# A run of four row gathers is put behind VectorE's one-hots of the next batch, three batches ahead, in place of TensorE's factors of the next batch, four ahead

## The chip, the cores and the metric

The kernel runs on one core of one Trainium2 chip. The core has five engines with queues of their own: PE (TensorE, matmuls), DVE (VectorE), ACT (ScalarE), POOL (GpSimd) and SP (SyncE, which here only issues transfers). The metric is the time of the program on the device in microseconds, the median of several executions.

## The reference

One message-passing block of a graph network, then a layer norm over the sum of the input and the block's output. There are 1250 nodes with 512 values each (384 of them three-component vectors `v`, 128 scalars `s`), and 40000 edges, sorted by their target node `dst`.

```python
x_j = x[src]
v_j = x_j[:, :384].reshape(E, 128, 3)
s_j = silu(x_j[:, 384:] @ W1 + b1) @ W3 + b3
edge_basis = rbf * cutoff @ W2 + b2
split = s_j * edge_basis
s1, s2, s3 = (split[:, :128], split[:, 128:256], split[:, 256:])
v_msg = v_j * s1[:, :, None] + s3[:, :, None] * edge_attr1[:, None, :]
msg = jnp.concatenate([v_msg.reshape(E, 384), s2], axis=1)
x = x + jax.ops.segment_sum(msg, dst, num_segments=N_NODES)
```

After this first sum each node's new row is put through an update (matrices `U`, `V`, `Wu1`, `Wu2`), and a second sum adds the updated rows over the same edges. What the second sum adds depends on the source node alone.

## The kernel before

**Tiling.** `windowed()` does the whole work. The edges are cut into 79 chunks of 512, four chunks make a group, and there are 20 groups. A group is worked on in four batches; a batch has one tile of 128 edges from each of its chunks, so four tiles in nearly all batches, three in batch 76 and two in the last three. There are NT = 80 batches and 313 tiles. An edge needs one row of a table in DRAM, which was made beforehand for every node: 640 values, the vector part with the scalar part after its two matmuls.

**The loop.** Step t of the loop at L1677 stands for batch t. What the steps do around the change, in the order of the program:

- `messages(t)` (DVE): L899 and L901 multiply the gathered rows by the edges' factors, in place, in the room where the rows were put. Then come `make_pair(t)` (L919), `make_hot(t + 1)` (L830, a one-hot matrix of the edges' targets within a 16-node window, for the next batch) and `make_spread(t + 1)` (L842, the same times the edge's direction).
- `run(first, t)`: work that a planner has set down for this step, of node blocks and of the second sum. `run(early)`, `run(mid)`, `run(late)` and `run(dve)` are more of it, further on in the step.
- `add_messages(t - 1)` and `count_links(t - 1)` (PE): matmuls of the one-hots with the messages of the batch before, L935 and L941, and of link counts for the second sum, L964.
- `edge_factors(t + 1)` (PE, L889): eight matmul records for four tiles into one set of PSUM banks, named `eb`. There is one such set, so these matmuls wait until L901 of batch t has read it. L899 of batch t + 1 waits for them.
- `gather(t + 4, made)`: a run of four indirect DMAs on POOL's queue (L739), each of 128 rows. `made` is the last matmul of `edge_factors(t + 1)`, and the run's first gather has a dependency on it that is written by hand (L748); the other three stand behind the first in POOL's queue.

The gathered rows go to five rooms in turn, three in the buffer `more` and two in `nodes`, which is why the profile lists L739, L899 and L901 under two names. The gathers of batches 0 to 3 are issued ahead of the loop, without a dependency by hand, and so are those of the last two batches at their places.

**What else sets the order.** The program's order is each engine's order. Across engines an instruction waits for what it reads and for the last reader of what it writes; only the dependencies by hand are added. `after_factors` (L1053) makes SP's transfers of node parts wait for `made` as well, the newest factors at the time when they are put into the program. POOL has other work near the end alone: a memset, casts of link counts, sums of parts of the output.

Of the kernel before, what the change touches and what calls it, by code (L numbers as in the profile page):

```python
# [64 lines left out]
def gnn_resnorm(  # L65
# [315 lines left out]
    with tc.If(misses_v == 0):  # L381
        windowed(tc, sh)
# [201 lines left out]
def windowed(tc, sh):  # L584
# [13 lines left out]
    nc = tc.nc  # L598
# [12 lines left out]
    def lanes(g, i, j):  # L611

        c = g * CPG + j
        if c >= NCH:
            return 0
        n = CHUNK if c < NCH - 1 else last_rows
        return max(0, min(P, n - i * P))
# [3 lines left out]
    NT = len(batches)  # L621

    def tiles(g, i):
        return [j for j in range(CPG) if lanes(g, i, j)]

    def runs(g, i):

        out = []
        for j in tiles(g, i):
            if out and lanes(g, i, out[-1][-1]) == lanes(g, i, j):  # L630
                out[-1].append(j)
            else:
                out.append([j])
        return [(slice(js[0], js[-1] + 1), len(js), lanes(g, i, js[0])) for js in out]
# [13 lines left out]
    with tc.tile_pool(  # L648
# [80 lines left out]
        sync = mybir.DependencyInfo(mybir.DependencyClass.Sync, mybir.DependencyReason.DATA)  # L729

        rooms = itertools.cycle(sh.rooms)

        def gather(t, behind=None):

            g, i = batches[t]
            rows_t = next(rooms)
            for j in tiles(g, i):
                n = lanes(g, i, j)
                got = nc.gpsimd.indirect_dma_start(  # L739
                    out=rows_t[:n, j, :],  # L740
                    out_offset=None,
                    in_=sh.table1,
                    in_offset=bass.IndirectOffsetOnAxis(
                        ap=sh.src_i[:n, g, i * CPG + j : i * CPG + j + 1], axis=0
                    ),
                )
                if behind is not None and j == 0:
                    tc.add_manual_dep(  # L748
                        got.ins, behind.ins.name, sync,
                        reason="so that rows come while PE is ahead of DVE",  # L750
                    )
            clear_rest(t, rows_t, nc.gpsimd)
            rows_of[t] = rows_t
# [59 lines left out]
        def clear_rest(t, tile, engine=nc.vector):  # L813
            g, i = batches[t]
            for j in tiles(g, i):
                m = lanes(g, i, j)
                if m < P:
                    engine.memset(tile[m:, j], 0.0)

        def make_hot(t):  # L820

            g, i = batches[t]
            hots[t] = pool.tile([P, CPG, WIN], F32, name="hot", bufs=3)
            spread[t] = pool.tile([P, CPG, 3, WIN], F32, name="spread", bufs=3)
            clear_rest(t, hots[t])
            clear_rest(t, spread[t])
            for js, n, m in runs(g, i):
                e = i * CPG + js.start
                shape = [m, n, WIN]
                nc.vector.tensor_tensor(  # L830
                    hots[t][:m, js, :],
                    lane[:m, None, :WIN].to_broadcast(shape),
                    sh.local[:m, g, e : e + n, None].to_broadcast(shape),
                    op=ALU.is_equal,
                )

        def make_spread(t):
            g, i = batches[t]
            for js, n, m in runs(g, i):
                e = i * CPG + js.start  # L840
                shape = [m, n, 3, WIN]
                nc.vector.tensor_mul(  # L842
                    spread[t][:m, js],
                    hots[t][:m, js, None, :].to_broadcast(shape),
                    sh.attr[:m, g, e : e + n, :, None].to_broadcast(shape),
                )
# [11 lines left out]
        def mark_sources(t):  # L858

            g, i = batches[t]  # L860
            for j in tiles(g, i):
                e = g * EPG + i * CPG + j
                one = onehots[t][:, j, :]
                nc.scalar.activation(  # L864
                    one, one, AF.Relu, scale=less[:, e : e + 1], bias=worth[:, e : e + 1]
                )
# [5 lines left out]
        def new_banks(name, sizes):  # L872

            factor_banks.close()
            banks.push(factor_banks)
            of = factor_banks.enter_context(tc.tile_pool(name=name, bufs=1, space=PSUM))
            return [
                of.tile([P, n, BANK], F32, name=f"{name}_{k}") for k, n in enumerate(sizes)
            ]

        def factors_of(t, js):

            return made_in[t][:, js]

        def edge_factors(t):
            g, i = batches[t]
            for j in tiles(g, i):
                rows = slice(j * FEAT, j * FEAT + N_RBF + 1)
                made = nc.tensor.matmul(  # L889
                    made_in[t][:, j, :V], turned[g][rows, i, :], sh.w2_sb[rows, :],  # L890
                    start=True, stop=True,
                )
            return made

        def messages(t):
            g, i = batches[t]
            msg = rows_of.pop(t)
            for js, n, m in runs(g, i):
                nc.vector.tensor_mul(msg[:m, js, V:], msg[:m, js, V:], factors_of(t, js)[:m, :, C:V])  # L899
            for js, n, m in runs(g, i):  # L900
                nc.vector.tensor_mul(  # L901
                    msg[:m, js, :V].rearrange("p t (k c) -> p t k c", k=3),
                    msg[:m, js, :V].rearrange("p t (k c) -> p t k c", k=3),
                    factors_of(t, js)[:m, :, None, :C].to_broadcast([m, n, 3, C]),
                )
            make_pair(t)
            if t + 1 < NT:
                make_hot(t + 1)
                make_spread(t + 1)
            msgs[t] = msg  # L910

        def make_pair(t):

            g, i = batches[t]
            pair = pool.tile([P, CPG, PARTS * WIN], F16, name="pair", bufs=2)
            for js, n, m in runs(g, i):
                e = g * EPG + i * CPG + js.start
                shape = [m, n, PARTS * WIN // 2, 2]
                nc.vector.tensor_tensor(  # L919
                    pair[:m, js, :].rearrange("p t (l h) -> p t l h", h=2),  # L920
                    number[:m, : PARTS * WIN].rearrange("p (l h) -> p l h", h=2)[
                        :, None
                    ].to_broadcast(shape),
                    column[:m, e : e + n, None, :].to_broadcast(shape),
                    op=ALU.is_equal,
                )
            pairs[t] = pair
# [688 lines left out]
        def run(when, step):  # L1616
            for _, fn, args in sorted(when.get(step, []), key=lambda task: task[0]):
                fn(*args)
# [49 lines left out]
            at(early, 4 * g - 3, 6, bring_fades, g)  # L1668
        distances(0)
        mark_sources(0)  # L1670
        ahead = 4
        for t in range(min(ahead, NT)):
            gather(t)
        edge_factors(0)
        make_hot(0)
        make_spread(0)
        for t in range(max(*first, *early, *late, *dve, *mid) + 1):  # L1677
            if t < NT:
                messages(t)
            if t == NT - 4:  # L1680
                assert all(len(tiles(*batches[u])) == CPG // 2 for u in range(NT - 3, NT))
                made_in[NT - 3], made_in[NT - 2] = new_banks("halves", [CPG // 2] * 2)
                made_in[NT - 1] = made_in[NT - 3]
            if t == NT - 1:
                out_banks.update(zip(in_factors, new_banks("out", [1] * CPG), strict=True))
            run(first, t)
            if 1 <= t <= NT:
                add_messages(t - 1)
                count_links(t - 1)
            run(early, t)  # L1690
            if t + 1 < NT - 2:
                made = edge_factors(t + 1)
            if t + 1 in (NT - 3, NT - 2):
                edge_factors(t + 2)
            if t + ahead < NT:
                gather(t + ahead, made if t + ahead < NT - 2 else None)
            run(mid, t)
            run(late, t)
            run(dve, t)
# [368 lines left out]
```

## Time and profile before

| | us |
|---|---|
| median of 3 executions | 582.91 (582.26 to 584.65) |
| the profiled execution | 581.79 |
| its span, from the first to the last instruction | 579.9 |
| first L899 into the room `nodes` | 62.8 |
| last L899 into the room `nodes` | 518.1 |

The mean granted clock of TensorE was 0.902 in the profiled execution. A row of a timeline has the start of an instruction in us from the span's start, its duration in us, the engine, the line, the operation with out<-in and the tile's shape, and in brackets how long the engine was idle before it and what ended that. A group's row has the count, the busy time, the mean duration in ns, and the idle time before its instructions with the most frequent releaser. A row of a window has its two ends, its length, the busy time and count of each engine in the order PE, PE's weight loads, DVE, ACT, POOL (or of one engine alone), TensorE's granted clock, the DMA engines' busy share and GB/s. Ends of matmuls are modelled, so what follows a matmul is read from the waiting instruction's start.

### The profile page before, as it was taken

To read this page: it belongs to the slowest core of one execution; us is meant where nothing else is said; L and a number is where in the kernel's file an instruction comes from. 1 tells how busy PE (TensorE), PEld (TensorE's weight loads), DVE (VectorE), ACT (ScalarE), POOL (GpSimd) and SP (SyncE) were. 2 spreads that over 40 slices of the span, in tenths; PEclk is the share of its full clock that TensorE was granted. 3 is DMA by queue.
4 is the path that set the end of the run, shared out by engine and by line. 5 is a ranking of instruction groups with operands and counts; after the bars stand their busy time and mean duration, and the time that the engine had idled before them with its cause. 6 is when DMAs were issued, how large, how long until landed. Compare 5 with 4: busy or idle time off the path is not lost.

```text
span 579.9 us, 11213 instructions
## 1 busy us (share of the span) xinstructions
PE 458.1 (79%) x4233; PEld 254.6 (44%) x4233; DVE 437.1 (75%) x680; ACT 372.5 (64%) x946; POOL 332.9 (57%) x361
## 2 busy tenths in 40 slices
PE   6566777769768778977778697889789887989993
PEld 3322432335335334534434353454445444445682
DVE  6893778767776877778778867788778686878775
ACT  3470466557656676856667685677668675877664
POOL 6375666655555656656566655566565655653530
PEclk9956787889887998989799889889989998999998
DMA  7986777775766777777677777777777776765514
GB/s 225 303 239 213 212 233 213 213 227 172 237 191 192 235 223 216 216 241 208 201 230 224 216 218 207 223 222 244 224 225 200 247 234 194 230 198 185 189 37 148
DMA packets 37937, 123.28 MB, mean 213 GB/s; under 512 B 7296, under 2 KB 9870, under 8 KB 37874
## 3 DMA queue, kind: packets, MB, share of 16 engines
q0 software_dynamic: 25824, 104.47, 60.5%
q1 hardware_dynamic: 10574, 17.24, 9.0%
q10 hardware_dynamic: 1476, 0.77, 0.5%
q8 instruction: 35, 0.57, 0.4%
q14 instruction: 28, 0.23, 0.1%
HBM read 112.94 MB, written 9.51 MB: 211 GB/s over the span
## 4 chain that ended last, share of the span: by engine, by line
PE 32%; POOL 21%; issue 17%; DVE 14%; DMA 8%; ACT 5%; another core or an unknown queue 2%; DVEq 0%; POOLq 0%; ACTq 0%; SPq 0%
POOL more L739 12%; POOL nodes L739 7%; PE agg L935 6%; PE eb L889 6%; PE agg L941 4%; PE begun L1339 4%; DMA more<-table,src_i 3%; DMA nodes<-table,src_i 3%; DVE nodes L901 2%; DVE more L901 2%; PE adj L964 2%; PE work L806 2%; DVE nodes L899 2%; DVE more L899 2%
## 5 line engine op out<-in xcount | busy, mean ns | idle before, releaser
L739 POOL DMA_INDIRECT more<-table,src_i x189 | 183.9, 973 | 127.1 <-issue 46.2
L739 POOL DMA_INDIRECT nodes<-table,src_i x124 | 119.3, 962 | 80.0 <-issue 28.7
L864 ACT ACTIVATE one<-one,weight,src_f 128x128 f16<-128x128 f16 x313 | 128.5, 482 | 0.4 <-issue 0.2
L889 PE MATMUL eb<-w_sb,basis_t 21*128 21x384 f32 x614 | 83.2, 561 | 42.9 <-issue 18.3
L854 ACT ACTIVATE one<-number,low 128x128 f16<-128x128 f16 x313 | 99.7, 391 | 5.5 <-remote 3.9
L901 DVE TENSOR_TENSOR more<-more,eb 128x1536 f32<-128x1536 f32 (+2 forms) x48 | 81.8, 1705 | 0.0
L899 DVE TENSOR_TENSOR more<-more,eb 128x1024 f32<-128x1024 f32 (+2 forms) x48 | 57.0, 1190 | 31.3 <-PE eb L889 13.5
L935 PE MATMUL agg<-more,hot 128*32 128x512 f32 x378 | 67.1, 697 | 3.3 <-ACT sums L986 2.1
L889 PEld LDWEIGHTS eb<-w_sb,basis_t 21*128 21x128 f32 x614 | 28.2, 189 | 69.5 <-issue 33.5
L941 PEld LDWEIGHTS agg<-more,spread 128*32 128x32 f32 x1134 | 42.6, 122 | 35.8 <-issue 34.3
L941 PE MATMUL agg<-more,spread 128*32 128x128 f32 x1134 | 53.2, 300 | 2.0 <-issue 1.9
L901 DVE TENSOR_TENSOR nodes<-nodes,eb 128x1536 f32<-128x1536 f32 x30 | 52.4, 1747 | 0.0
L935 PE MATMUL agg<-nodes,hot 128*32 128x512 f32 x248 | 44.0, 688 | 6.2 <-ACT sums L986 3.8
L842 DVE TENSOR_TENSOR spread<-hot,carried 128x384 f32<-128x384 f32 (+1 forms) x81 | 44.0, 544 | 2.8
L899 DVE TENSOR_TENSOR nodes<-nodes,eb 128x1024 f32<-128x1024 f32 x30 | 36.5, 1216 | 11.7 <-DMA more<-table,src_i 8.2
L964 PE MATMUL adj<-pair,one 128*128 128x160 f16 x313 | 39.0, 249 | 2.5 <-issue 2.5
L1010 DVE SCALAR_TENSOR_TENSOR counts<-counts,adj 128x320 f16<-128x320 f16 x20 | 9.7, 486 | 40.9 <-ACT counts L1004 28.8
L941 PEld LDWEIGHTS agg<-nodes,spread 128*32 128x32 f32 x744 | 28.0, 123 | 25.5 <-issue 25.1
L919 DVE TENSOR_TENSOR pair<-number,column 128x640 f16<-128x640 f16 (+1 forms) x81 | 38.2, 472 | 0.0
L941 PE MATMUL agg<-nodes,spread 128*32 128x128 f32 x744 | 35.7, 302 | 2.4 <-issue 2.4
L811 ACT COPY basis_t<-work 128x512 f32<-128x512 f32 x20 | 11.7, 586 | 35.9 <-PE work L806 32.6
L964 PEld LDWEIGHTS <-one 128*128 128x128 f16 x313 | 24.0, 107 | 15.0 <-issue 13.4
(274 smaller groups left out, 717.6 us busy)
## 6 DMA issues: line engine op xcount, KB each, us to landing
table<-more SPq DMA_DIRECT2D x10, 320.0 KB
more<-table,src_i POOLq DMA_INDIRECT x189
spilled<-begun SPq DMA_DIRECT2D x10, 256.0 KB
more<-spilled SPq DMA_DIRECT2D x2, 1280.0 KB
node_x<-in_x_dram SPq DMA_DIRECT2D x35, 64.0 KB
nodes<-table,src_i POOLq DMA_INDIRECT x124
out_dram<-more SPq DMA_DIRECT2D x7, 256.0 KB
nodes<-in_x_dram POOLq DMA_DIRECT2D x2, 768.0 KB
```

Of the source, the lines that this page charges most:

```text
L739: got = nc.gpsimd.indirect_dma_start(out=rows_t[:n, j, :], out_offset=None, in_=sh.table1, in_offset=bass.IndirectOffsetOnAxis(ap=sh.src_i ...
L842: nc.vector.tensor_mul(spread[t][:m, js], hots[t][:m, js, None, :].to_broadcast(shape), sh.attr[:m, g, e : e + n, :, None].to_broadcast(sh ...
L854: nc.scalar.activation(onehots[t][:, j, :], number[:, :P], AF.Abs, bias=low[:, e : e + 1])
L864: nc.scalar.activation(one, one, AF.Relu, scale=less[:, e : e + 1], bias=worth[:, e : e + 1])
L889: made = nc.tensor.matmul(made_in[t][:, j, :V], turned[g][rows, i, :], sh.w2_sb[rows, :], start=True, stop=True,)
L899: nc.vector.tensor_mul(msg[:m, js, V:], msg[:m, js, V:], factors_of(t, js)[:m, :, C:V])
L901: nc.vector.tensor_mul(msg[:m, js, :V].rearrange("p t (k c) -> p t k c", k=3), msg[:m, js, :V].rearrange("p t (k c) -> p t k c", k=3), fac ...
L919: nc.vector.tensor_tensor(pair[:m, js, :].rearrange("p t (l h) -> p t l h", h=2), number[:m, : PARTS * WIN].rearrange("p (l h) -> p l h", ...
L935: nc.tensor.matmul(agg[j * WIN : (j + 1) * WIN, :], hots[t][:, j, :], msg[:, j, :width], start=(i == 0), stop=False, skip_group_check=True,)
L941: nc.tensor.matmul(agg[j * WIN : (j + 1) * WIN, c * C : (c + 1) * C], spread[t][:, j, c, :], msg[:, j, width:], start=False, stop=(i == la ...
L964: nc.tensor.matmul(to[:, :, at : at + WIN], one[:m, j, :], pair[:m, j, :].rearrange("e (p n) -> e p n", n=WIN), start=(i == 0 and j == js[ ...
L1339: nc.tensor.matmul(acc, casts[a, b], rows[:, a, :], start=(start and a == first and k == 0), stop=(stop and a == end - 1 and k == 1),)
```

## The change

A run of gathers is moved within the step, from behind `edge_factors(t + 1)` to right behind `messages(t)`. Its first gather depends on two instructions: `made`, which is at that place the last matmul of `edge_factors(t)`, and `gate`, the one-hots that `make_hot(t + 1)` makes on DVE. The run in step t is that of batch t + 3, not t + 4, and three runs stand ahead of the loop, not four. The last two batches' runs have no dependency by hand, as before. `messages` and `make_hot` return the instruction for it.

```diff
-        def gather(t, behind=None):
+        def gather(t, behind=()):
...
-                if behind is not None and j == 0:
+                for made in behind if j == 0 else ():
                     tc.add_manual_dep(
-                        got.ins, behind.ins.name, sync,
-                        reason="so that rows come while PE is ahead of DVE",
+                        got.ins, made.ins.name, sync,
+                        reason="so that rows come while PE makes a batch's factors",
                     )
...
-                nc.vector.tensor_tensor(
+                made = nc.vector.tensor_tensor(
                     hots[t][:m, js, :],
...
+            return made
...
+            gate = None
             make_pair(t)
             if t + 1 < NT:
-                make_hot(t + 1)
+                gate = make_hot(t + 1)
                 make_spread(t + 1)
             msgs[t] = msg
+            return gate
...
-        ahead = 4
+        ahead = 3
         for t in range(min(ahead, NT)):
             gather(t)
-        edge_factors(0)
+        made = edge_factors(0)
         make_hot(0)
         make_spread(0)
         for t in range(max(*first, *early, *late, *dve, *mid) + 1):
             if t < NT:
-                messages(t)
+                gate = messages(t)
+            if t + ahead < NT:
+                gather(t + ahead, (made, gate) if t + ahead < NT - 2 else ())
...
             if t + 1 in (NT - 3, NT - 2):
                 edge_factors(t + 2)
-            if t + ahead < NT:
-                gather(t + ahead, made if t + ahead < NT - 2 else None)
```

## The prediction

> **What bounds the kernel now.** I read the page's busy shares first, then its costliest groups, and last the timelines of PE, DVE and POOL over two steps in the middle.
>
> ```profile
> span 579.9 us, 11213 instructions
> PE 458.1 (79%) x4233; PEld 254.6 (44%) x4233; DVE 437.1 (75%) x680; ACT 372.5 (64%) x946; POOL 332.9 (57%) x361
> L739 POOL DMA_INDIRECT more<-table,src_i x189 | 183.9, 973 | 127.1 <-issue 46.2
> L739 POOL DMA_INDIRECT nodes<-table,src_i x124 | 119.3, 962 | 80.0 <-issue 28.7
> L899 DVE TENSOR_TENSOR more<-more,eb 128x1024 f32<-128x1024 f32 (+2 forms) x48 | 57.0, 1190 | 31.3 <-PE eb L889 13.5
> L899 DVE TENSOR_TENSOR nodes<-nodes,eb 128x1024 f32<-128x1024 f32 x30 | 36.5, 1216 | 11.7 <-DMA more<-table,src_i 8.2
> ```
>
> No engine is full, and DVE's idle time in front of L899 (31.3 + 11.7 us) is put down to PE's factors (`eb`) in one group and to a gather in the other. So the question is what sets the length of a step. The windows, all engines first and then L899 alone, give its mean:
>
> ```profile
> 63.00:518.00 455.00, 366.24 (x3665) 198.44 (x3669) 346.75 (x486) 305.84 (x786) 274.48 (x285) 0.91 0.73 218
> 63.00:518.00 455.00, 86.24 (x71) 0.91 0.73 218
> ```
>
> 71 steps in 455 us are 6.41 us each; DVE works 346.75/71 = 4.88 us of that. Three timelines of one step, DVE's, PE's and POOL's:
>
> ```profile
> 287.07 1.22 DVE L899 TENSOR_TENSOR nodes<-nodes,eb 128x1024 f32<-128x1024 f32 x1 [0.60 <-DMA more<-table,src_i]
> 288.21 1.75 DVE L901 TENSOR_TENSOR nodes<-nodes,eb 128x1536 f32<-128x1536 f32 x1
> 290.28 0.28 DVE L830 TENSOR_TENSOR hot<-lane,carried 128x128 f32<-128x128 f32 x1
> 293.25 1.22 DVE L899 TENSOR_TENSOR nodes<-nodes,eb 128x1024 f32<-128x1024 f32 x1 [1.31 <-DMA more<-table,src_i]
> ```
>
> ```profile
> 286.08 0.93 PE L889 MATMUL eb<-w_sb,basis_t 21*128 21x384 f32 x8
> 290.21 0.93 PE L889 MATMUL eb<-w_sb,basis_t 21*128 21x384 f32 x8
> ```
>
> ```profile
> 287.31 0.94 POOL L739 DMA_INDIRECT more<-table,src_i  x1 [3.16 <-PE eb L889]
> 291.05 0.94 POOL L739 DMA_INDIRECT more<-table,src_i  x1 [0.30 <-issue]
> 293.49 0.94 POOL L739 DMA_INDIRECT more<-table,src_i  x1 [1.49 <-remote]
> 299.55 0.94 POOL L739 DMA_INDIRECT nodes<-table,src_i  x1 [1.39 <-remote]
> ```
>
> The factors started at 286.08 let L899 go at 287.07, 0.99 us later, with no gather under way. The same eight matmuls started at 290.21, inside a run of gathers (287.31 to 291.05 + 0.94 = 291.99), let L899 go only at 293.25, 3.04 us later: 1.26 us after the run's last gather and 5.94 us after its first. That L899's own rows had been asked for four steps before; the "DMA" named as its releaser is the last event, not the cause. I read it so: **PE's signals are held while a run's rows stream, until about 5.9 us after the run's start.** The run in its turn starts 0.24 us after the factors' release (287.31 less 287.07). So a quiet step is a closed loop of 0.25 + 5.9 = 6.15 us: factors, run, held factors (287.07, 293.25, and runs at 293.49 and 299.55, 6.06 apart).
>
> Is 5.9 us the stream's own price? At the start 20 gathers are issued without a stop:
>
> ```profile
> 26.86 1.21 POOL L739 DMA_INDIRECT more<-table,src_i  x1 [9.07 <-DMA u_sb<-in_L_gnn_U_dram]
> 52.20 0.95 POOL L739 DMA_INDIRECT nodes<-table,src_i  x1 [0.30 <-issue]
> 56.34 1.22 DVE L899 TENSOR_TENSOR more<-more,eb 128x1024 f32<-128x1024 f32 x1 [9.01 <-PE eb L889]
> 48.44 0.79 PE L889 MATMUL eb<-w_sb,basis_t 21*128 21x384 f32 x1 [1.15 <-issue]
> 55.51 0.79 PE L889 MATMUL eb<-w_sb,basis_t 21*128 21x384 f32 x1 [0.42 <-issue]
> ```
>
> From 26.86 to 56.34 are 29.5 us, so at most 1.47 us a gather and 5.9 us for four. PE crawls there: eight factor matmuls spread from 48.44 to 55.51, and DVE stands idle 9.01 us.
>
> **The change part by part.** *The wait.* The new run waits for the one-hots of the next batch. L830 ends 290.28 + 0.28 - 287.07 = 3.49 us after L899 starts; with the 0.25 us to POOL's start as above, the run starts 3.75 us after L899 instead of 0.24. Behind the waiting gather stand on POOL the run's other three and the later runs, nothing else before the tail. The other wait, for this step's factors, is met already, since L899 needed them: 0. The run is put ahead of PE's work of the step in the program, but POOL's own queue holds the same gathers in the same order in the loop: 189 + 124 = 313 gathers, before and after, 291.99 - 287.31 = 4.68 us a run, and with the 0.30 between two gathers 4.98 from run to run at the least. The next factors start after L901 (288.21 + 1.75 = 289.96) at 290.21 at the earliest, and would signal 0.99 later, some 3.9 to 4.1 us after L899, which is 0.2 to 0.4 us after the new run's start. There the stream has hardly begun, the first gather's 0.94 us being still under way, and I take them to be released on time. So the next L899 no longer waits for the end of this run.
>
> *What is late next.* DVE has 4.88 us a step, POOL 4.98, the stream 5.9. If the stream is the next bound, a step is 5.9: it loses the 0.25 us between factors and run, which the new gate takes out of the loop, since the one-hots come (3.75 us) well before the last run has been served. Below that stand 4.98 (POOL), above it 6.15 (no gain), and beyond that a hold, priced with the rivals. I take 5.9, the row at the start being the nearest to runs without a gap.
>
> *The steps that gain.* In 14 of the 71 steps the factors start over 1.1 us after L901, since PE waits for chains of other work. The first and the last of the 14, L901 and then the factors:
>
> ```profile
> 113.61 1.75 DVE L901 TENSOR_TENSOR more<-more,eb 128x1536 f32<-128x1536 f32 x1
> 486.83 1.75 DVE L901 TENSOR_TENSOR nodes<-nodes,eb 128x1536 f32<-128x1536 f32 x1
> 116.47 1.48 PE L889 MATMUL eb<-w_sb,basis_t 21*128 21x384 f32 x8
> 491.38 0.93 PE L889 MATMUL eb<-w_sb,basis_t 21*128 21x384 f32 x8
> ```
>
> The factors start 1.11 us after L901's end (113.61 + 1.75) in the first and 2.80 in the last. There the chain sets the step, and I count no gain: 71 - 14 = 57 steps x 0.25 = 14.2 us.
>
> *Three batches ahead.* A run that starts 3.75 us after L899 has landed 5.9 us later, at 9.65; its rows are wanted three steps on, at 3 x 5.9 = 17.7. Cover 8 us: 0. Should steps fall to 4.98, it is still 5. The start needs rows of its own:
>
> ```profile
> 39.92 0.28 DVE L830 TENSOR_TENSOR hot<-lane,carried 128x128 f32<-128x128 f32 x1
> 43.16 0.95 POOL L739 DMA_INDIRECT nodes<-table,src_i  x1 [0.31 <-issue]
> 59.54 0.28 DVE L830 TENSOR_TENSOR hot<-lane,carried 128x128 f32<-128x128 f32 x1
> 76.31 1.21 DVE L899 TENSOR_TENSOR more<-more,eb 128x1024 f32<-128x1024 f32 x1
> ```
>
> Batch 3's gathers begin at 43.16 behind batch 2's; the one-hots that they will wait for, of batch 1, end at 40.20: 0. Run 5 waits for those of batch 3, so it starts at 59.82 + 0.25 = 60.1 and not when PE's factors came (56.34); it lands near 66, and its batch is wanted at 76.31: 0. SP's transfers keep their wait on `made` (L1053), which is assigned at the same place: 0. In the tail the last runs stay without a gate, and come one step later in number but earlier in the step; POOL's casts behind them shift by at most one run of two, from 0 to 2.2 us: I take 0. The added names and the tuple make no instruction.
>
> *A page against it.* The Trainium skill, "DMA: Bandwidth & Descriptors", Anatomy of one DMA — SWDGE (gpsimd) path, gives about 2.0 us plus bytes/436e3 for a DMA of this kind; the 327,680 bytes of a gather (128 rows of 640 values, a quarter of L899's and L901's 1024 + 1536) would stream in 0.75 us, an estimate, and four in 3.0. By it the stream would not bind, and a step would be POOL's 4.98. The 1.47 us at the start speak against that.
>
> **Sum.** The profiled execution took 581.79 us, 1.9 around its span of 579.9, and stands 1.1 under the median of 582.91. 581.8 - 14.2 = 567.6; on the median **568.7 us**.
>
> **The rivals.**
>
> *Slower: the new run holds the factors it was to let pass.* The point from which it decides: a signal that comes over about 1.1 us after the run's start is held to 5.9 us after it, so that L899 to L899 is 3.75 + 5.9 = 9.65 instead of 6.15, 3.5 us more. The 14 late steps lie there. At 1.11 late the price is 3.5; at 2.80 it is 9.65 - (3.92 + 2.80) = 2.9; at 3.0 in the mean 14 x 3.0 = 42, and 568.7 + 42 = **611**. It breaks even at 14.2/3.5 = 4 steps. And two runs without a gap hold both ways, as this pair of runs shows:
>
> ```profile
> 162.56 1.19 POOL L739 DMA_INDIRECT more<-table,src_i  x1 [0.30 <-issue]
> 164.06 0.95 POOL L739 DMA_INDIRECT more<-table,src_i  x1 [0.30 <-issue]
> 163.84 1.21 DVE L899 TENSOR_TENSOR nodes<-nodes,eb 128x1024 f32<-128x1024 f32 x1
> 164.98 1.75 DVE L901 TENSOR_TENSOR nodes<-nodes,eb 128x1536 f32<-128x1536 f32 x1
> 170.15 1.70 PE L889 MATMUL eb<-w_sb,basis_t 21*128 21x384 f32 x8 [1.08 <-issue]
> 171.88 1.22 DVE L899 TENSOR_TENSOR more<-more,eb 128x1024 f32<-128x1024 f32 x1 [0.40 <-PE eb L889]
> ```
>
> The second run comes 0.30 us behind the first, PE's factors start 3.4 us after L901's end (164.98 + 1.75), and the step is 8.04 us. If every third quiet step went so, 57/3 x (8.04 - 6.15) = 36 us more. For it: both rows are there. Against it: between them lie steps in which the factors, at 0.2 to 0.4 us into the run, are before the point.
>
> *No change: the 6.15 us are PE's own.* PE is the busiest engine, and its records' ends are modelled; if its backlog and not the stream holds the factors, moving the run does nothing: **583**. The Trainium skill speaks for it: "SBUF — State Buffer", Who interferes with whom, says that DMA never contends with a compute engine and that PE never waits on anyone. Against it: the trace's 0.99 us without a run, 3.04 within one. The case that the change doesn't do what it says, because POOL is gated by something else, ends here too.
>
> *Much faster: the stream is quicker than 1.47 us.* In the loop the run's end follows its last gather by 1.26 us only, so the rows may keep pace with POOL's issue. Then a step is 4.98: 57 x 1.17 = 67, 581.8 - 67 + 1.1 = **516**. Against it: the start.
>
> *Rows late.* Needs 8 us lost; no row shows such a stretch.
>
> **How the numbers follow.** Forecast (558 to 577) 0.35; much faster or between (505 to 558) 0.14; no change 0.14; slower, by either hold, 0.36 (590 to 611 + 36 = 647); rows late 0.01. A measurement of this kernel tells about 0.5% from no change. Faster 0.49, within 0.5% 0.14, slower 0.37. The range from 540 to 618 leaves out the far end of the fast case, some 0.08, and of the slow one, some 0.12. Both signs hold much, so the likeliest case's own range stands here again: 558 to 577.
>
> **What would show it.** Right: L739's runs start 3.75 us after L899 and have factors as releaser no more; L899 follows the factors' start by 1.0 us; the mean step is near 6.2. The slow rival: steps of 9 to 10 us beside steps of 5, factors 3 us or more from start to L899, PE's matmuls single with gaps put down to "issue". No change: steps of 6.15, with L889 as late as now although no run is under way. Much faster: POOL's gap between runs at 0.30. The forecast falls if held signals are released by something other than the run's end.

## The result, and the profile after

The changed kernel took 695.69 us (median of 4 runs, 690.63 to 698.76) against 583.78 us before (median of 4), a ratio of 1.191 with an interval of 1.183 to 1.199. It is slower by 112 us; 568.7 us had been forecast. The profiled execution took 698.76 us.

The page of the changed kernel, its span, the busy shares and four of its groups (L900 and L902 are the old L899 and L901, L890 the old L889):

```profile
span 697.0 us, 11213 instructions
PE 520.5 (75%) x4233; PEld 271.4 (39%) x4233; DVE 436.8 (63%) x680; ACT 371.0 (53%) x946; POOL 334.4 (48%) x361
L739 POOL DMA_INDIRECT more<-table,src_i x189 | 184.2, 974 | 207.4 <-issue 116.2
L739 POOL DMA_INDIRECT nodes<-table,src_i x124 | 120.2, 970 | 116.2 <-issue 88.5
L900 DVE TENSOR_TENSOR more<-more,eb 128x1024 f32<-128x1024 f32 (+2 forms) x48 | 57.0, 1190 | 68.7 <-remote 35.7
L900 DVE TENSOR_TENSOR nodes<-nodes,eb 128x1024 f32<-128x1024 f32 x30 | 36.6, 1219 | 39.2 <-remote 22.1
```

DVE and POOL do the same work in the same time as before (436.8 against 437.1 us, 334.4 against 332.9). What grew is idle time: in front of L900 it went from 31.3 + 11.7 = 43.0 to 68.7 + 39.2 = 107.9 us, in front of two other DVE instructions of the planned work, L762 and L797, from 13.5 + 20.7 = 34.2 to 39.9 + 45.7 = 85.6, and in front of the gathers from 207.1 to 323.6. So no work of DVE or POOL became dearer; they wait longer. PE's records did grow, from 458.1 to 520.5 us, at a granted clock of 0.810 in place of 0.902. The clock alone would make them 458.1 x 0.902/0.810 = 510, an estimate that takes a record to grow as the clock falls. From the first L900 in the room `nodes` to the last the windows say:

```profile
62.80:633.80 571.00, 427.36 (x3658) 214.84 (x3659) 346.41 (x487) 304.25 (x785) 275.27 (x285) 0.80 0.58 174
```

571 us for the 71 steps that took 455 before: 8.04 us a step in place of 6.41, 116 us in all, out of the 117 by which the two profiled spans differ. How one gets there is seen in DVE's, POOL's and PE's timelines over three steps:

```profile
360.72 1.22 DVE L900 TENSOR_TENSOR more<-more,eb 128x1024 f32<-128x1024 f32 x1 [5.99 <-remote]
363.92 0.28 DVE L830 TENSOR_TENSOR hot<-lane,carried 128x128 f32<-128x128 f32 x1
365.58 1.22 DVE L900 TENSOR_TENSOR more<-more,eb 128x1024 f32<-128x1024 f32 x1
368.78 0.28 DVE L830 TENSOR_TENSOR hot<-lane,carried 128x128 f32<-128x128 f32 x1
376.65 1.22 DVE L900 TENSOR_TENSOR more<-more,eb 128x1024 f32<-128x1024 f32 x1 [5.74 <-remote]
381.65 1.22 DVE L900 TENSOR_TENSOR nodes<-nodes,eb 128x1024 f32<-128x1024 f32 x1
```

```profile
364.95 1.14 POOL L739 DMA_INDIRECT nodes<-table,src_i  x1 [5.65 <-issue]
368.90 0.99 POOL L739 DMA_INDIRECT nodes<-table,src_i  x1 [0.30 <-issue]
370.19 0.95 POOL L739 DMA_INDIRECT nodes<-table,src_i  x1 [0.30 <-issue]
373.95 0.95 POOL L739 DMA_INDIRECT nodes<-table,src_i  x1 [0.30 <-issue]
380.88 0.95 POOL L739 DMA_INDIRECT more<-table,src_i  x1 [5.98 <-PE eb L890]
```

```profile
363.65 1.66 PE L890 MATMUL eb<-w_sb,basis_t 21*128 21x384 f32 x8 [1.30 <-DVE more L902]
371.76 1.27 PE L890 MATMUL eb<-w_sb,basis_t 21*128 21x384 f32 x8
379.59 0.93 PE L890 MATMUL eb<-w_sb,basis_t 21*128 21x384 f32 x8 [0.54 <-DVE more L902]
```

Most steps come in pairs: 33 of the 71 are over 9 us, 11.19 in the mean, and the other 38 take 5.31 in the mean. The step from 360.72 is short, 4.86 us: its factors pass as the run starts, and DVE goes on without a wait. The next is 11.07 us. Its run's wait is over at 368.78 + 0.28 = 369.06, while POOL is still issuing the run before, so the two stand 0.30 us apart (368.90 + 0.99 to 370.19). The factors for 376.65 belong into that stretch of eight gathers and are let go 1.75 us after its last one (373.95 + 0.95). Then POOL has been idle 5.98 us, the next run starts alone, and the pair begins again: 15.93 us for two steps, against 12.3 for two quiet steps before.

### The profile page after: what moved, and what is told of

Its sections match the earlier page's. It is cut to its first block, busy times and chain, and to the rows that moved or that the text cites. A ratio compares the mean times of both kernels' runs of the same rounds, so it can differ in the third digit from the quotient of the medians.

```text
span 697.0 us, 11213 instructions
## 1 busy us (share of the span) xinstructions
PE 520.5 (75%) x4233; PEld 271.4 (39%) x4233; DVE 436.8 (63%) x680; ACT 371.0 (53%) x946; POOL 334.4 (48%) x361
## 5 line engine op out<-in xcount | busy, mean ns | idle before, releaser
L890 PE MATMUL eb<-w_sb,basis_t 21*128 21x384 f32 x614 | 99.5, 600 | 35.0 <-issue 14.0
L900 DVE TENSOR_TENSOR more<-more,eb 128x1024 f32<-128x1024 f32 (+2 forms) x48 | 57.0, 1190 | 68.7 <-remote 35.7
L902 DVE TENSOR_TENSOR more<-more,eb 128x1536 f32<-128x1536 f32 (+2 forms) x48 | 81.8, 1705 | 0.0
L938 PE MATMUL agg<-more,hot 128*32 128x512 f32 x378 | 72.9, 753 | 3.0 <-ACT sums L989 2.3
L944 PE MATMUL agg<-more,spread 128*32 128x128 f32 x1134 | 61.7, 315 | 17.3 <-issue 17.3
L900 DVE TENSOR_TENSOR nodes<-nodes,eb 128x1024 f32<-128x1024 f32 x30 | 36.6, 1219 | 39.2 <-remote 22.1
L890 PEld LDWEIGHTS eb<-w_sb,basis_t 21*128 21x128 f32 x614 | 34.5, 206 | 66.5 <-issue 32.9
L902 DVE TENSOR_TENSOR nodes<-nodes,eb 128x1536 f32<-128x1536 f32 x30 | 52.4, 1748 | 0.0
L944 PE MATMUL agg<-nodes,spread 128*32 128x128 f32 x744 | 43.2, 329 | 11.2 <-issue 11.0
L938 PE MATMUL agg<-nodes,hot 128*32 128x512 f32 x248 | 49.9, 800 | 1.9 <-ACT sums L989 1.6
L811 ACT COPY basis_t<-work 128x512 f32<-128x512 f32 x20 | 11.7, 586 | 71.4 <-remote 51.2
L944 PEld LDWEIGHTS agg<-nodes,spread 128*32 128x32 f32 x744 | 30.5, 135 | 46.4 <-issue 45.3
L967 PE MATMUL adj<-pair,one 128*128 128x160 f16 x313 | 41.9, 257 | 5.4 <-issue 5.2
L1034 PE MATMUL work<-sums,sel 128*128 128x512 f32 x36 | 27.9, 887 | 14.6 <-remote 10.3
L797 DVE TENSOR_TENSOR basis<-turn,adj 128x320 f32<-128x320 f32 x19 | 9.2, 486 | 45.7 <-remote 40.8
```

The lines of the kernel that those rows point to most:

```text
L890: made = nc.tensor.matmul(made_in[t][:, j, :V], turned[g][rows, i, :], sh.w2_sb[rows, :], start=True, stop=True,)
L902: nc.vector.tensor_mul(msg[:m, js, :V].rearrange("p t (k c) -> p t k c", k=3), msg[:m, js, :V].rearrange("p t (k c) -> p t k c", k=3), fac ...
L938: nc.tensor.matmul(agg[j * WIN : (j + 1) * WIN, :], hots[t][:, j, :], msg[:, j, :width], start=(i == 0), stop=False, skip_group_check=True,)
L944: nc.tensor.matmul(agg[j * WIN : (j + 1) * WIN, c * C : (c + 1) * C], spread[t][:, j, c, :], msg[:, j, width:], start=False, stop=(i == la ...
L967: nc.tensor.matmul(to[:, :, at : at + WIN], one[:m, j, :], pair[:m, j, :].rearrange("e (p n) -> e p n", n=WIN), start=(i == 0 and j == js[ ...
L1034: nc.tensor.matmul(blks[b], sh.sel[:, k, :], sums.pop(2 * b + k), start=(k == 0), stop=(k == 1))
```

## The experiments

**The kernel's two parts apart.** The changed kernel without the new wait, at the new place and with the shorter lead:

```diff
-                gather(t + ahead, (made, gate) if t + ahead < NT - 2 else ())
+                gather(t + ahead, (made,) if t + ahead < NT - 2 else ())
```

> The changed kernel without the wait for the one-hots: the run of batch t + 3 waits for this step's factors alone, as the run of batch t + 4 did in the step before. Theory (PE's signals are held while rows stream, and the later start lets two runs touch): the loop of the kernel before comes back, a run 0.25 us after each factors' release, quiet steps of 6.1 to 6.2 us, 580 to 587 us. Rival A (the shorter lead, three batches): still near 690, with DVE waiting for rows. Rival B (the new place in the program, ahead of PE's work of the step): still over 640.

576.5 us against 576.66 for the kernel before, ratio 1.0005 (0.9967 to 1.0044). The place in the program and the new numbering cost nothing; rivals A and B fall as far as this lead goes. The run of batch t + 3 behind the factors of t is the run that the kernel before put behind the factors of t + 1 for t + 4, so this kernel is the one before in other words, and the whole loss hangs on the one wait for the one-hots.

The other part alone, the kernel before with a shorter lead:

```diff
-        ahead = 4
+        ahead = 3
```

> The kernel before with three batches ahead instead of four; place and wait as before. Theory: only the lead shrinks by a step, from about 15 us to 9 us between a run's end and its L899; rows still land in time: 580 to 590 us. Rival A (lead): over 620, L899 released by the gather of its own batch.

572.98 us, ratio 0.9955 (0.9912 to 0.9999). A step less of lead doesn't cost, it gains a little. It was run again on another chip:

> The kernel before with three batches ahead, again, for its interval: the first 16 gathers instead of 20 are issued without a stop at the start, so L899 of batch 3 starts some 5 us earlier; 0.990 to 0.998 of the kernel before if that is all, 1.00 if the gain at the start is lost later.

580.99 us against 585.83, ratio 0.9933 (0.9905 to 0.9962): faster than both kernels on the chips where a run of gathers holds PE's signals (below stands one that shows no such hold). L899 of batch 3 in the first of these two runs, and the same instruction in the changed kernel without the new wait, on one chip:

```profile
57.01 1.22 DVE L899 TENSOR_TENSOR nodes<-nodes,eb 128x1024 f32<-128x1024 f32 x1
```

```profile
61.49 1.21 DVE L900 TENSOR_TENSOR nodes<-nodes,eb 128x1024 f32<-128x1024 f32 x1
```

The 4.5 us between them come from the start, where one run fewer is issued without a stop, and they cover the gain (3.7 us there).

**The start of the run at another point of the step.** The wait on L899 of the same step in place of the one-hots (L900 in this file):

```diff
-                nc.vector.tensor_mul(msg[:m, js, V:], msg[:m, js, V:], factors_of(t, js)[:m, :, C:V])
+                gate = nc.vector.tensor_mul(msg[:m, js, V:], msg[:m, js, V:], factors_of(t, js)[:m, :, C:V])
...
-            gate = None
...
-                gate = make_hot(t + 1)
+                make_hot(t + 1)
```

> The changed kernel with the wait on L899 of the same step in place of the next one-hots. L899 ends 1.2 us after its start and the wait has cost up to 0.75 us, so a run starts some 2.0 us after L899, and the next factors (signal at 3.9 to 4.1 at the earliest) fall 2 us into it. Theory: every one of them is held to the run's end, no run touches the next; equal steps of 2.0 + 5.9 = 7.9 us, none of 5 us and few of 11: 660 to 700 us. Rival C (time grows with the delay of the run's start, 112 us for 4.2 us): 112 x 2.0/4.2 = 53, about 637 us.

642.03 us, ratio 1.110 (1.100 to 1.120). By its total this is nearest to rival C, whose 53 us would make 630 on this chip, a ratio of 1.092; the theory's figure was too high. DVE's, POOL's and PE's timelines, though, show held factors and runs that touch, and not steps that are all slower by the same:

```profile
334.57 1.21 DVE L900 TENSOR_TENSOR more<-more,eb 128x1024 f32<-128x1024 f32 x1
341.85 1.22 DVE L900 TENSOR_TENSOR more<-more,eb 128x1024 f32<-128x1024 f32 x1 [1.95 <-remote]
346.85 1.22 DVE L900 TENSOR_TENSOR nodes<-nodes,eb 128x1024 f32<-128x1024 f32 x1
355.85 1.21 DVE L900 TENSOR_TENSOR nodes<-nodes,eb 128x1024 f32<-128x1024 f32 x1
```

```profile
336.06 0.95 POOL L739 DMA_INDIRECT nodes<-table,src_i  x1 [5.15 <-DVE more L900]
343.33 0.94 POOL L739 DMA_INDIRECT more<-table,src_i  x1 [2.58 <-DVE more L900]
348.34 0.95 POOL L739 DMA_INDIRECT more<-table,src_i  x1 [0.30 <-DVE nodes L900]
```

```profile
339.21 0.93 PE L890 MATMUL eb<-w_sb,basis_t 21*128 21x384 f32 x8
344.79 0.93 PE L890 MATMUL eb<-w_sb,basis_t 21*128 21x384 f32 x8 [0.69 <-DVE more L902]
```

A run starts 1.49 us after L900 (336.06 less 334.57), not 2.0, since this wait costs only 0.28 us. The factors of 339.21 start 3.15 us into this run and are let go 5.79 us after its start (341.85), so the step is 7.28. The next step is 5.00: its factors start 1.46 us into the run (344.79 less 343.33) and were let go in mid-run, which the theory had ruled out, and then the runs at 343.33 and 348.34 touch and the third step is 9.00. The three make 7.09 a step. The whole trace says the same: where the factors start less than 1.6 us after the first gather of a run, or of runs that touch, L900 starts before the last gather's end in 20 of 22 steps; where they start later, L900 starts after that end in 44 of 47. So in this trace a run has a first part in which factors pass, and the theory put its end too early.

**The run in two halves**, the first two gathers behind the factors alone, the last two behind the one-hots:

```diff
-                for made in behind if j == 0 else ():
+                for made in behind[j // 2 : j // 2 + 1] if j % 2 == 0 else ():
```

> The changed kernel with the run in two halves: the first two gathers wait for this step's factors alone, the last two for the one-hots of the next batch. Theory: the first half is served by about 3.2 us after L899, the second starts at about 4.2, so the factors (3.9 to 4.1) pass between them and the next step starts 4.8 us later; then the halves touch, but a hold ends after 2 to 4 gathers and not after 8. Mean step 6.0 to 6.8, 565 to 615 us. Rival B (place) or C (delay): half of the 112 us, near 640.

595.96 us, ratio 1.031 (1.024 to 1.038). That is inside the theory's range, and no gain over the kernel before. In the trace the gathers stand mostly in stretches of two and of six (55 and 27 stretches): a second half runs into both halves of the next run. That is more than the two to four gathers that the theory had, and less than eight; the mean step is 6.6 us.

**What holds PE's signals.** First the bytes. Each gather fetches 320 values of a row in place of 640, the rest of the rooms is zeroed at the start, so part of the messages is left out:

```diff
-                    out=rows_t[:n, j, :],
+                    out=rows_t[:n, j, : V // 2 + C],
-                    in_=sh.table1,
+                    in_=sh.table1.rearrange("n (h f) -> (n h) f", h=2),
...
+        for room in sh.rooms:
+            nc.vector.memset(room[:, :, V // 2 + C :], 0.0)
```

> The kernel before with gathers of half a row: 320 of the 640 values of each row are fetched (of another node's row), the other half of the rooms is zeroed once at the start and stays so, which leaves out part of the messages. The number of gathers, of descriptors' rows and of POOL's instructions stays, the bytes halve. Theory S (PE's signals are held by the streaming of the bytes): the rows of a gather take some 0.75 us in place of 1.47, so the hold ends about 0.7 us earlier behind the run's last gather, or PE's signals pass in the gaps between gathers: quiet steps of 5.0 to 5.5 us, 510 to 555 us with some 7 us of zeroing. Theory I (held by POOL's issue of the gathers): 5.9 us as before, 575 to 595 us.

> The same half rows in the changed kernel, with its wait for the one-hots. Theory S: a run is served as fast as POOL issues it, runs 0.30 us apart leave PE gaps, and the pairs of a 5-us and an 11-us step disappear: 500 to 570 us. Theory I: runs still touch on POOL, the pairs stay: 680 to 710 us.

587.47 us (ratio 1.003, 1.000 to 1.006) and 698.72 us (1.194, 1.187 to 1.201). Half the bytes change nothing in either kernel. Two rows of L899 and the window of the kernel before with half rows:

```profile
294.56 1.22 DVE L899 TENSOR_TENSOR nodes<-nodes,eb 128x1024 f32<-128x1024 f32 x1 [1.28 <-PE work L1163]
300.63 1.22 DVE L899 TENSOR_TENSOR more<-more,eb 128x1024 f32<-128x1024 f32 x1 [1.20 <-remote]
```

```profile
63.00:518.00 455.00, 366.12 (x3651) 196.07 (x3647) 344.76 (x483) 304.13 (x782) 271.79 (x283) 0.90 0.42 116
```

The DMA engines' share falls from 0.73 to 0.42, 116 GB/s in place of 218, and a quiet step still takes 6.07 us. Theory S, the one of the prediction, falls: the 5.9 us are no price of bytes. What they are is seen in the held steps. In the kernel before, 27 times DVE stands idle for factors that started inside a run of four, and L899 starts 0.68 to 1.32 us after the end of the run's last gather, 1.2 in the median; with half rows there are 22 such steps, 0.86 to 1.29, and 1.2 again. POOL's 4.68 us for four gathers and these 1.2 make the 5.9.

Then the gathers themselves. Each is replaced by a plain transfer of 128 whole rows from SP's queue, with the same waits and bytes. The rows are not those of the edges; the lookup is left out:

```diff
-                got = nc.gpsimd.indirect_dma_start(
-                    out=rows_t[:n, j, :],
-                    out_offset=None,
-                    in_=sh.table1,
...
+                first = (4 * t + j) % 9 * P
+                got = nc.sync.dma_start(rows_t[:n, j, :], sh.table1[first : first + n, :])
```

> The changed kernel with each gather replaced by a plain transfer of 128 whole rows of the table from SP's queue, at the same place, into the same room, with the same waits and bytes; the rows are not those of the edges, so the lookup is left out. Theory I (POOL's issue of gathers holds PE's signals, not the rows that stream): no hold, factors signal 1 us after their start, no pairs of 5 and 11 us; DVE's 4.9 us and PE's 5.2 us a step bind: 470 to 560 us. Theory T (any stream of rows into the rooms holds PE): pairs or steps over 6 us stay, over 600 us.

> The same plain transfers from SP's queue in the kernel before. Theory I: the wait for the factors then costs nothing, within 3% of the run above, 470 to 560 us. Theory T: 575 to 590 us.

And the gathers with half the rows, 64 in place of 128 (the lower half of the rooms zeroed as above):

```diff
-                n = lanes(g, i, j)
+                n = lanes(g, i, j) // 2
```

> The changed kernel with gathers of 64 rows in place of 128: the lower half of each room is zeroed once at the start and stays so, which leaves out half of the edges' messages. As many gather instructions, half the descriptors and bytes. Theory D (the hold goes by descriptors, one a row): the hold behind a run shrinks and the pairs get shorter, under 640 us. Theory N (it goes by the number of gather instructions): 680 to 710 us, as with half rows.

These three shared a chip on which the kernel before took 484.72 us, not the 576.66 and 585.83 of the two chips of the runs above. They gave 463.34 us (0.956, 0.951 to 0.962), 462.58 (0.955, 0.946 to 0.963) and 480.49 (0.989, 0.986 to 0.993), and tell nothing of a hold, if that chip has none. The changed kernel, the kernel before and two of the three were run on one more chip:

> The changed kernel as it is. The last three runs fell on a chip on which the kernel before took 484.7 us and gathers of 64 rows showed factors 1 us after their start, with runs 0.30 us apart: no hold there. If this chip holds PE's signals (the kernel before at 575 to 590 us): 690 to 700 us again. If it does not: theory I says that the hold is the whole loss, so the wait for the one-hots costs nothing where POOL's queue is never empty: 480 to 490 us, within 1.5% of the kernel before. Rival (the wait itself costs, hold or none): 5% or more slower there too.

> The kernel before as it is, for a trace on the same chip as its neighbours here. If the chip does not hold PE's signals: factors signal about 1 us after their start, runs 0.30 us apart on POOL, steps of 5.0 us, DVE near 90% busy, about 485 us. If it does: 575 to 590 us with steps of 6.15 us.

> Plain transfers of 128 whole rows from SP's queue in place of the gathers, in the changed kernel; the lookup is left out. Its first run fell on the chip without a hold (463 us), where it can't tell the theories apart. If this chip holds: theory I (POOL's issue of gathers holds PE's signals) 455 to 480 us, no pairs of steps; theory T (any stream of rows into the rooms) over 600 us. If it does not hold: 463 us again, and nothing follows.

> Gathers of 64 rows in place of 128 in the changed kernel, half of the edges' messages left out. If this chip holds: theory D (the hold goes by descriptors, one a row) under 640 us; theory N (by the number of gather instructions) 680 to 710 us. If it does not hold: 480 us again.

This chip holds PE's signals. The changed kernel took 696.14 us (1.190, 1.174 to 1.207) and the kernel before 584.27. Plain transfers gave 462.94 us (0.792, 0.782 to 0.801), what they gave on the chip without a hold; gathers of 64 rows gave 704.5 (1.205, 1.191 to 1.219), where the other chip had 480.49; their mean step here is 8.05 us, that of the changed kernel 8.02. The window of the plain transfers in the changed kernel, on the holding chip:

```profile
63.00:400.00 337.00, 306.58 (x3570) 170.49 (x3569) 331.85 (x475) 295.42 (x767) 0.63 (x1) 0.98 0.87 289
```

The rows arrive at 289 GB/s, more than in any run with gathers, and DVE is busy 331.85 of 337 us. So the stream of rows from SP's queue holds nothing, and neither bytes nor rows set the length of the hold. What is left of the causes tried is the gathers that POOL issues. Two in place of four, with plain transfers for the other two tiles, so that runs need not touch:

```diff
+                if j >= CPG // 2:
+                    first = (4 * t + j) % 9 * P
+                    nc.sync.dma_start(rows_t[:n, j, :], sh.table1[first : first + n, :])
+                    continue
                 got = nc.gpsimd.indirect_dma_start(
```

> The changed kernel with two gathers in a run instead of four; the other two tiles of a batch come by plain transfers of whole rows from SP's queue, so the lookup is left out for half of the edges. A run then takes POOL 2.2 us and holds PE's signals some 3.1 us. It starts 4.0 us after L899 and the next L899 follows 4.8 us after the last, so runs lie 1.7 us apart after a hold has ended. If this chip holds (the kernel before at 575 to 590 us): theory (the loss comes from runs that touch) 460 to 500 us, no step of 11 us; rival (the start after the one-hots costs by itself, in proportion to the gathers) half the way from 463 to 696, about 580. If it does not hold: 460 to 490, and nothing follows.

467.91 us on a chip where the kernel before took 575.48 (0.811, 0.795 to 0.827). POOL, DVE and PE (the gather is L743 in this file, L899 is L904, the factors are L894):

```profile
254.11 0.95 POOL L743 DMA_INDIRECT more<-table,src_i  x1 [3.06 <-PE eb L894]
255.36 0.94 POOL L743 DMA_INDIRECT more<-table,src_i  x1 [0.30 <-issue]
258.50 0.94 POOL L743 DMA_INDIRECT nodes<-table,src_i  x1 [2.20 <-PE work L810]
```

```profile
254.27 1.22 DVE L904 TENSOR_TENSOR more<-more,eb 128x1024 f32<-128x1024 f32 x1
259.00 1.22 DVE L904 TENSOR_TENSOR more<-more,eb 128x1024 f32<-128x1024 f32 x1
263.75 1.22 DVE L904 TENSOR_TENSOR more<-more,eb 128x1024 f32<-128x1024 f32 x1
```

```profile
252.95 0.93 PE L894 MATMUL eb<-w_sb,basis_t 21*128 21x384 f32 x8
257.55 0.93 PE L894 MATMUL eb<-w_sb,basis_t 21*128 21x384 f32 x8
```

With 2.2 us of POOL's time free between runs the same wait for the one-hots does no harm: steps of 4.73 and 4.75 us, and of the 71 steps in the trace one is over 6.5 us, of 7.18. The factors start ahead of their run here (252.95 and 254.11, 257.55 and 258.50), so this run shows that the pairs go when runs don't touch; how long two gathers hold a signal it doesn't show.

**The change without a hold.** The changed kernel again, on the chip of the run just above and on the one where the kernel before took 484.72 us:

> The changed kernel as it is. If this chip does not hold PE's signals (the kernel before near 485 us): 480 to 490 us by the theory, 5% or more slower than before by the rival that the wait itself costs. If it holds: 690 to 700 us again.

> The changed kernel as it is, for a chip that does not hold PE's signals (the kernel before near 485 us there): 480 to 490 us if the loss exists only with the hold, 5% or more slower than before if the wait for the one-hots costs by itself. On a chip that holds: 680 to 700 us, and nothing new follows.

The first chip holds PE's signals: 682.69 us, 1.183 (1.165 to 1.202). On the second nothing is held: **483.75 us against 483.95**, ratio 1.001 (0.997 to 1.006). Its PE, POOL and DVE timelines:

```profile
281.40 0.93 PE L890 MATMUL eb<-w_sb,basis_t 21*128 21x384 f32 x8 [0.19 <-DVE more L902]
```

```profile
278.12 1.25 POOL L739 DMA_INDIRECT nodes<-table,src_i  x1 [0.30 <-issue]
283.67 0.95 POOL L739 DMA_INDIRECT nodes<-table,src_i  x1 [0.30 <-issue]
284.93 0.94 POOL L739 DMA_INDIRECT more<-table,src_i  x1 [0.30 <-PE agg L944]
```

```profile
283.23 1.21 DVE L900 TENSOR_TENSOR nodes<-nodes,eb 128x1024 f32<-128x1024 f32 x1
288.69 1.21 DVE L900 TENSOR_TENSOR nodes<-nodes,eb 128x1024 f32<-128x1024 f32 x1
```

Gathers run on and on, 0.30 us apart, and factors that start at 281.40 in the midst of them have L900 going at 283.23, as soon as DVE is free. Runs that touch cost nothing there. POOL never stops for a wait in this trace: it is idle 0.63 us at most before any gather behind the first, and its runs follow each other every 5.16 us, close to the 4.98 that the prediction had as POOL's own least. DVE is busy 344.33 of the 367.20 us from the first to the last L900 in `nodes`.

## Why the prediction was wrong

**The mechanism was seen, and its consequence not drawn.** That PE's factors are late while a run of gathers is under way was seen on every chip but one. The prediction also had right that the factors, due 3.9 to 4.1 us after L899, would now pass at the start of the run. In the changed kernel they do, in about every other step.

**The step that failed is "What is late next".** It said: "If the stream is the next bound, a step is 5.9: it loses the 0.25 us between factors and run". A step of 5.9 us needs factors that come every 5.9 us, and nothing in the new order makes them. Once factors pass, the next L899 comes after DVE's work alone, 4.86 us later at 365.58; the next run follows POOL's queue at 0.30 us; and the factors after that fall into the middle of eight gathers, where by the prediction's own rule they must wait for the end. The sum should have followed two steps and not one: 4.86 + 11.07 = 15.93 us against 12.3, 1.8 us a step in the pairs, 1.63 over all 71 steps, 116 us. The rival on the slow side named this very thing ("two runs without a gap hold both ways") and showed the pair at 164 us. Its count and its price were both low: 57/3 = 19 steps of 8.04 us, where 33 steps of 11.19 in the mean came, so that its range ended at 647. Its point of decision, 1.1 us into a run, came too early: factors that start 1.45 us into a run, and signal 1 us later at the earliest, still passed in most steps of the kernel with the wait on L899.

**The steps that were to gain were too many.** The 0.25 us were counted for 57 quiet steps of 6.15 us. In the trace before, 27 of the 71 steps lie between 5.9 and 6.4 us, and 24 are over 6.5. This made the forecast gain too large and has nothing to do with its sign.

**The 5.9 us were read as a price of bytes.** "Is 5.9 us the stream's own price?" was answered with 29.5 us for 20 gathers. Half rows answer it with no: 0.42 of the DMA engines' time in place of 0.73, and the same step. The 5.9 us are POOL's own 4.68 for four gathers and some 1.2 us behind the last. The Trainium skill, "SBUF — State Buffer", Who interferes with whom, says that DMA never contends with a compute engine. The plain transfers agree, 289 GB/s into the same rooms with DVE busy all the time. Its further words, that PE never waits on anyone, don't fit the chips with a hold if they are read for PE's signals: gathers on POOL delayed these there.

**The terms at nothing.** The place in the program, the shorter lead and the start of the kernel cost nothing, as predicted (1.0005 for place and lead together; the lead alone gains 0.5 to 0.7%, at the start). The wait itself was put at 0.25 us to POOL's start; in the pairs it takes 0.75 (364.20 to 364.95), which isn't what decides.

**The rival "no change"** (583 us) names the outcome on one chip of five, though neither its time nor its reason: there nothing is held, and POOL's queue, which issues without a stop, sets the step, with DVE busy 94% of the time.

What stays open: why one chip lets PE's signals pass and the others don't, and by what path gathers on POOL delay them. The runs show that a hold lasts until about 1.2 us after a run of four, that plain transfers from SP's queue make none, and that bytes and rows don't set its length. They don't tell apart the number of gather instructions, the time that POOL spends on them (0.95 us for one, 0.90 with 64 rows, in the median) and the queue that they use. The clock was granted lower with the change (0.827 against 0.887 on one chip), but on that chip the plain transfers had 0.96; it was lower wherever signals were held, and it was not tried by itself.

## What to carry to other kernels

Where a trace shows that one engine's signals come late during another's bursts, a change of when the burst starts must be followed over several steps, until the pattern repeats: a burst that no longer waits for the late signal can run into the next burst, and then a signal waits for both. A wait that looks useless, as this run's wait for the factors did, may be what keeps bursts apart. And before a stretch is called the price of bytes, halve the bytes and look at the stretch again.

## What the runs showed of the hardware

On four chips the kernel before took 575 to 586 us, on a fifth 484. The changed kernel's trace on the fifth shows PE's factors on time among gathers. On two of the four it shows them late, as do traces of its variants on the other two; the chip of the first measurement, 583.78 and 695.69 us, is not known. The kernel before was not traced on the fifth. A program that is tuned around a delay on one chip may be tuned for nothing on another: the change costs 18 to 19% where it was measured with a hold, and 0.1% without one, within its interval. Plain transfers in place of the gathers, without the lookup, give 463 us on both kinds of chip, 4% less than the kernel before on the one and 21% less on the other.
